# Second step of a graph layer on one core: the finished tile scaled on GpSimd, the threshold guess kept as a logarithm, the last sum taken out earlier

## The chip, the cores and the metric

The kernel runs on one core of a Trainium2 chip. The core has a matrix engine (TensorE, "PE" in the profile), a vector engine (VectorE, "DVE"), a scalar engine (ScalarE, "ACT"), a general engine (GpSimd, "POOL") and a queue that only starts transfers (SyncE, "SP"). Each engine works through its own queue of instructions in order and waits on semaphores for the others. The metric is the time of the whole program on the device in microseconds, as the median of several runs.

## The reference

The layer takes 3327 nodes with 256 features and a sparse adjacency matrix (about 0.12% of the entries, and the diagonal). It normalises the features, mixes them in two steps, adds the result to its input and normalises again. Each step mixes in two ways: `R`, the fixed adjacency with normalised rows, and `A`, a full attention matrix of which every row keeps only its largest entries, those that together hold 90% of the row's sum.

```python
def _top_p_attention(X, W1, W2, W3):
    q = X @ W1.T @ W2.T
    k = X @ W3.T
    probs = softmax(q @ k.T / TAU)
    idx = argsort(-probs)
    sp = take_along_axis(probs, idx)
    cs = cumsum(sp)
    keep_sorted = cs - sp < TOP_P                 # TOP_P = 0.9
    mask = zeros(bool).at[rows, idx].set(keep_sorted)
    A = probs * mask
    return A / maximum(A.sum(-1, keepdims=True), 1e-12)
...
R = S + eye(N);  R = R / R.sum(-1, keepdims=True)
Xf = Xa = X
for n in range(STEPS):                            # STEPS = 2
    A = _top_p_attention(Xa, W1, W2, W3)
    Xf = R @ Xf
    Xa = A @ Xa
    Z = Z + Xf @ U1[n].T + Xa @ U2[n].T
h = X + Z
return (h - mu) / sqrt(var + LN_EPS) * ln_g + ln_b    # mu, var of each row of h
```

The layer's input `X` is `relu(layernorm(x))`, and its output is added to `x`.

## The kernel before, in words

**Tiles.** The 3327 nodes are padded to 3328, which makes 26 tiles of 128 rows. A tile's attention weights `e` are 128 x 3328 in float32, and four to six such tiles lie on the chip at a time. One round of the program works on several tiles, each at another stage; a round of the second step finishes one tile.

**What is done with a tile in the second step.**
- `weights` makes the logits with TensorE (L598) and their exponentials with ScalarE (L602, L606), which also adds up the row sums `Z`.
- `measured_twice` guesses, for each row, a threshold below which the entries hold a little less than a tenth of `Z`. It starts from a first guess `col(9)` out of moments of the row (`guessed`, L618 to L623), and makes three passes of ScalarE over the whole tile (L631, called by `through`): one adds up how far entries lie below the guess, one counts them, and a third counts them below a better guess, `col(13)`. Between these passes stand chains of operations on 128 x 1 columns, spread over ScalarE, VectorE and GpSimd. The better guess is the first one times a factor (L684 to L686). The last guess `col(16)` is `col(13)` times a power (L709, L712); where the measured mass shows that the guess is out of its range (L711), 1e30 is added, so that the proof at the end fails and a slow, exact program runs instead.
- `settle` makes one pass of VectorE that keeps only the entries below `col(16)` (L726), finds the eight largest of each of 20 segments (the scan, twenty MAX8 at L731), sorts the 48 largest of those (L738, L740), finds from their running sum the exact cut (L745 to L750), and makes a second pass of VectorE that sets everything under the cut to zero (L760).
- `Sums` turns the tile round in seven groups of up to four blocks (L806, copied out by ScalarE at L808) and multiplies them with the features `xw` into the accumulator `pa` (L820). There is one buffer for `pa`.
- `diffuse` and `spread` do the sparse mixing with `R`: rows that GpSimd gathers by index (L898, five gathers for a tile), multiplied at L906 and added at L1088.
- `finish` takes `pa` out and adds it to the rest (L930), computes mean and deviation of the rows (L456, L457, L463, L464, L938), scales the tile with ScalarE (L945), multiplies by the gain and adds the bias and the input on GpSimd (L946 to L948), and sends the tile off (L950).

**What sets the order.** The functions are generators, and each `yield` ends a piece. For every round and each of its seven parts, a string of letters in `PLAN` says which generators are moved on by one piece: `d` is `settle` and `c` the same of the tile before; `m` is `measured_twice` of the next tile and `n` of the tile after its round; `s` is `spread`, `f` is `finish`, `g` a gather, `w` and `q` parts of `weights`, `l` the laws of the moments. `OPEN` and `LAST` hold the strings of the first and last rounds. At the end every instruction of PE, ACT, DVE and (in the second step) POOL is tied to the one written ahead of it on its engine, so that the queues keep exactly this order; the SP queue's order is left to the scheduler.

Of the kernel before, what the change touches and what calls it, by code (L numbers as in the profile page):

```python
# [13 lines left out]
AF = mybir.ActivationFunctionType  # L14
ALU = mybir.AluOpType
# [7 lines left out]
NT = (N + P - 1) // P  # L23
# [287 lines left out]


BIG = 1.0e30
SEG = 168
NSEG = -(-NP // SEG)
ROUNDS = (5, 6)
# [27 lines left out]
def guess_graph_layer(ctx, tc, x, adj, w1t, w2t, w3t, u1t, u2t, ln_g, ln_b, out, flag):  # L344
# [15 lines left out]
    V, G, S, PE = nc.vector, nc.gpsimd, nc.scalar, nc.tensor  # L360
# [265 lines left out]
    def con(k):  # L626
        return one[:, k : k + 1]
# [5 lines left out]
    def measured_once(r):  # L633
# [25 lines left out]

        V.tensor_scalar(col(5), oa[:, 1:2], NP - 31.0, BIG, ALU.is_gt, ALU.mult)  # L660
        V.tensor_scalar(col(6), col(4), col(1), 0.35, ALU.mult, ALU.is_lt)
        V.scalar_tensor_tensor(col(5), col(6), BIG, col(5), ALU.mult, ALU.add)
        V.tensor_scalar(col(3), col(3), 1.0e20, col(9), ALU.min, ALU.mult)
        V.tensor_tensor(col(16), col(3), col(5), ALU.add)

    def measured_twice(r):
        e, ms = r["e"], r["ms"]

        col = guessed(r, small.tile([P, 18], F32, tag="g", name="g"))
        S.activation(col(1), col(0), AF.Exp, scale=-1.0, bias=con(5))
        S.activation(col(11), col(2), AF.Square, bias=con(4))  # L673
        G.tensor_scalar(col(11), col(11), ms(5), ms(6), ALU.mult, ALU.add)  # L674
        G.tensor_scalar(col(5), col(1), OFFSET[1], None, ALU.mult)
        yield
        oa = small.tile([P, 3], F32, tag="oa", name="oa")
        through(e, AF.Relu, col(9), -1.0, oa[:, 0:1])
        yield
        through(e, AF.Sign, col(9), -1.0, oa[:, 1:2])  # L680
        yield
        V.tensor_scalar(col(3), oa[:, 1:2], float(NP), col(9), ALU.add, ALU.mult)
        V.tensor_scalar(col(4), col(3), 0.5, oa[:, 0:1], ALU.mult, ALU.subtract)
        S.activation(col(6), col(4), AF.Ln, scale=col(1), bias=con(2))  # L684
        S.activation(col(6), col(6), AF.Exp, scale=col(11))
        S.activation(col(13), col(6), AF.Copy, scale=col(9))  # L686
        G.tensor_scalar(col(14), col(13), col(9), 0.25, ALU.add, ALU.mult)
        G.tensor_scalar(col(10), col(13), col(5), 1.0, ALU.mult, ALU.add)
        G.tensor_scalar(col(8), r["Z"], -0.1, col(4), ALU.mult, ALU.add)
        yield  # L690
        through(e, AF.Sign, col(13), -1.0, oa[:, 2:3])
        yield
        d1 = col(17)
        G.tensor_scalar(col(0), oa[:, 2:3], NP - 61.0, BIG, ALU.is_gt, ALU.mult)
        G.tensor_scalar(col(0), r["Z"], 0.035, col(0), ALU.mult, ALU.add)
        V.tensor_scalar(col(15), oa[:, 2:3], oa[:, 1:2], col(14), ALU.subtract, ALU.mult)
        V.tensor_scalar(d1, col(15), col(4), 0.0, ALU.add, ALU.max)

        S.activation(col(2), d1, AF.Abs, scale=col(1), bias=con(1))
        S.activation(col(2), col(2), AF.Ln, scale=0.2, bias=col(10))  # L700
        S.activation(col(3), d1, AF.Ln, scale=col(1), bias=con(2))
        S.activation(col(2), col(2), AF.Identity, scale=-1.0, bias=col(3))

        V.tensor_scalar(col(12), col(4), d1, 1.0e-30, ALU.subtract, ALU.add)
        V.reciprocal(col(12), col(12))
        G.tensor_scalar(col(12), col(12), col(8), 0.7, ALU.mult, ALU.max)
        G.tensor_scalar(col(11), col(12), 1.5, col(11), ALU.min, ALU.mult)
        yield
        S.activation(col(3), col(2), AF.Exp, scale=col(11))  # L709
        yield  # L710
        V.tensor_scalar(col(6), d1, col(0), BIG, ALU.is_lt, ALU.mult)  # L711
        V.tensor_scalar(col(16), col(3), col(13), col(6), ALU.mult, ALU.add)  # L712

    def measured(step, r):
        return measured_twice(r) if step else measured_once(r)
# [4 lines left out]
    def settle(step, t, r):  # L720
        e, col, Z = r["e"], r["col"], r["Z"]
        n = 8 * ROUNDS[step]
        d2 = small.tile([P, 1], F32, tag="d2", name="d2")
        need = small.tile([P, 1], F32, tag="need", name="need")
        w = scan.tile([P, NP], F32, tag="w", name="w")
        V.scalar_tensor_tensor(w, e, col(16), e, ALU.is_lt, ALU.mult, accum_out=d2)  # L726
        V.tensor_scalar(need, Z, -0.1, d2, ALU.mult, ALU.add)
        yield
        cand = small.tile([P, NSEG * 8], F32, tag="cand", name="cand", bufs=1)
        for s in range(NSEG):  # L730
            V.max(cand[:, 8 * s : 8 * s + 8], w[:, s * SEG : min(NP, (s + 1) * SEG)])  # L731
            if s in (NSEG // 2 - 1, NSEG - 1):
                yield
        at = lambda k: rec[:, step, k, t : t + 1]
        V.tensor_reduce(at(0), cand.rearrange("p (s k) -> p s k", k=8)[:, :, 7], AX.X, ALU.max)
        for k in range(ROUNDS[step]):
            b8 = bb[:, 1 + 8 * k : 9 + 8 * k]
            V.max(b8, cand)  # L738
            if k < ROUNDS[step] - 1:
                V.match_replace(cand, b8, cand, 0.0)  # L740
            if k == 2:
                yield
        b = bb[:, 1 : n + 1]
        cum = small.tile([P, TOPK], F32, tag="cum", name="cum", bufs=1)
        V.tensor_tensor_scan(cum[:, :n], bb[:, :n], bb[:, :n], 0.0, ALU.add, ALU.max)  # L745

        dr = small.tile([P, TOPK], F32, tag="dr", name="dr", bufs=1)
        V.tensor_scalar(dr[:, :n], cum[:, :n], need, None, ALU.is_ge)
        V.scalar_tensor_tensor(cum[:, :n], dr[:, :n], BIG, b, ALU.mult, ALU.add)
        V.tensor_reduce(at(1), cum[:, :n], AX.X, ALU.min)  # L750
        yield
        r["ra"] = ra = small.tile([P, 1], F32, tag="ra", name="ra")
        if t in (0, NT - 1):

            rb = small.tile([P, 1], F32, tag="rb", name="rb", bufs=1)
            for a, b_, r_ in ((0, FIRST, ra), (FIRST, NP, rb)):
                V.scalar_tensor_tensor(e[:, a:b_], e[:, a:b_], at(1), e[:, a:b_], ALU.is_ge, ALU.mult, accum_out=r_)  # L757
            V.tensor_tensor(ra, ra, rb, ALU.add)
        else:
            V.scalar_tensor_tensor(e, e, at(1), e, ALU.is_ge, ALU.mult, accum_out=ra)  # L760
        V.reciprocal(ra, ra)
        yield
        V.tensor_tensor(cum[:, :n], dr[:, :n], b, ALU.mult)
        V.tensor_reduce(at(2), cum[:, :n], AX.X, ALU.max)
# [164 lines left out]
    def finish(t, y, pa, ra):  # L929
        V.scalar_tensor_tensor(y, pa, ra, y, ALU.mult, ALU.add)  # L930
        yield
        mv = spread_of(y)
        yield
        xr = row.tile([P, D], F32, tag="xr", name="xr", bufs=1)
        nc.sync.dma_start(xr, x[t * P : (t + 1) * P])
        rstd = inverse(mv)
        nm = small.tile([P, 1], F32, tag="nm", name="nm")
        G.tensor_scalar(nm, mv[:, 0:1], rstd, -1.0, ALU.mult, ALU.mult)  # L938
        yield
        if t == NT - 1:  # L940
            G.tensor_tensor(xr, xr, bet, ALU.add)
            V.scalar_tensor_tensor(y, y, mv[:, 0:1], gam, ALU.subtract, ALU.mult)
            V.scalar_tensor_tensor(y, y, rstd, xr, ALU.mult, ALU.add)
        else:
            S.activation(y, y, AF.Identity, bias=nm, scale=rstd)  # L945
            G.tensor_tensor(y, y, gam, ALU.mult)  # L946
            G.tensor_tensor(xr, xr, bet, ALU.add)
            G.tensor_tensor(y, y, xr, ALU.add)  # L948
        h = min(P, N - t * P)
        nc.sync.dma_start(out[t * P : t * P + h], y[:h])  # L950
# [143 lines left out]
    def refetch(t):  # L1094
# [7 lines left out]


    PLAN = (("mdsssa", "mcdsssa", "edawwp", "msda", "mpdea", "gdawwq", "emgq"),
            ("llcmss", "lnms", "lwwnfd", "lcmdsssggggg", "fsmwqdf", "llmdf", "lmwd"))

    LAST = {NT - 1: ("cfss", "cn", "nd", "sss", "fdddddsf", "f", ""), NT: ("c", "", "", "ff", "ff", "fv", "f"),
            NT + 1: ("fv", "f", "", "", "f", "f", "f")}
    BEGIN = {-1: ("mba", "mmbba", "mwwbbaa", "bmwwb", "", "", ""),
             0: ("mdbba", "mcdbba", "medbwwbap", "mdabb", "mpdbwwba", "gdabbq", "q"),  # L1110
             1: ("mdsssbba", "mcdsssbba", "edbawwbp", "msdbga", "mpdea", "dawwq", "emgq")}
    OPEN = {-1: ("llcmss", "lnms", "lwwnfd", "lcmdsssggggg", "fmgswqdf", "llmdf", "lmwfdm"),
            0: ("cmssggg", "nms", "wwnfd", "cmdsss", "fsmgwqdf", "mdf", "mwd"),
            1: ("cmss", "nms", "wwnfd", "cmdsssggggg", "fsmwqdf", "mgdf", "mwd")}
    OPEN[2] = OPEN[3] = OPEN[1]
    fetching = itertools.chain(*(refetch(t) for t in range(NT)))
    LATE = (1, 4)
# [5 lines left out]
    for step in range(2):  # L1123
        sums = Sums(step, live, xw if step else x0, AHEAD[step])

        for i in range(-1, NT + 2):
# [4 lines left out]
            if step == 1 and i == -1:  # L1131
# [6 lines left out]
                c=work["d"],  # L1138
                d=settle(step, i, live[step, i]) if valid(i) else none,
                m=measured(step, live[step, i + 1]) if valid(i + 1) else none,  # L1140
                s=spread(step, i - 2 + 2 * step) if valid(i - 2 + 2 * step) else none,
# [97 lines left out]
```

## Time and profile before

| | |
|---|---|
| time before, median of 3 runs | 1396.95 us (1394.01 to 1402.68) |
| the profiled execution: its own time / its span | 1402.92 us / 1401.2 us |
| PE busy | 1276.6 us (91%) |
| DVE busy | 1199.8 us (86%) |
| ACT busy | 1102.5 us (79%) |
| POOL busy | 814.9 us (58%) |
| chain that ended last | DVE 43%, PE 41%, ACT 9% |

The profile is of one execution. A line of a group or of the timeline names the engine, the line of the program, the operation, what it writes and reads with the shapes, and its length; in brackets stands how long the engine stood idle before it and which instruction ended that. A line of the waits names who waited for whom, with the total in microseconds, how many times, and the longest. The chain that ended last is followed back from the last instruction to whatever released it. A busy share is an average over the whole span: the first step and the second differ, and the second, the one that is changed here, runs from about 780 us on.

### The profile page before, as it was taken

The numbers are of one execution on the slowest core, as the hardware profiler recorded it, in microseconds if no ns is written. First come the engines' busy times: TensorE is split into PE (matmuls) and PEld (weight loads), VectorE is DVE, ScalarE is ACT, GpSimd is POOL, SyncE is SP. The second block draws the span as 40 slices with busy tenths as digits, with TensorE's granted clock in tenths as the row PEclk, the third lists the DMA queues.
The fourth block names the chain that finished last, engine by engine and source line by source line (L and its number), as shares of the span: only waits on it lengthen the run. The fifth ranks groups of instructions, "written<-read, shape, count | busy, mean of one in ns | idle before, by whom it ended". The sixth has DMA issues, their size and how long they took to land.

```text
span 1401.2 us, 22108 instructions
## 1 busy us (share of the span) xinstructions
PE 1276.6 (91%) x6495; PEld 976.5 (70%) x6495; DVE 1199.8 (86%) x3689; ACT 1102.5 (79%) x2445; POOL 814.9 (58%) x1244
## 2 busy tenths in 40 slices
PE   5898899999999999999999769999999999999985
PEld 4535777777777777677677547777777777777764
DVE  6878788989999899889882589999998999999984
ACT  5566686778887788778764689999999999999941
POOL 6213888766777667566573475655645556555522
PEclk9999999999999999999999879999999999999998
DMA  8754454453444545444432221221322213122200
GB/s 290 242 167 141 126 153 132 124 148 111 140 142 127 140 117 151 124 126 134 114 82 79 62 63 53 79 84 53 91 61 75 79 58 91 57 79 80 57 20 22
DMA packets 92642, 149.77 MB, mean 107 GB/s; under 512 B 15425, under 2 KB 59072, under 8 KB 92512
## 3 DMA queue, kind: packets, MB, share of 16 engines
q1 hardware_dynamic: 75056, 105.37, 23.9%
q0 software_dynamic: 16640, 42.69, 12.3%
q8 instruction: 54, 0.88, 0.3%
q14 instruction: 76, 0.62, 0.1%
q10 hardware_dynamic: 816, 0.20, 0.1%
HBM read 120.93 MB, written 27.28 MB: 106 GB/s over the span
## 4 chain that ended last, share of the span: by engine, by line
DVE 43%; PE 41%; ACT 9%; issue 5%; POOL 1%; DMA 1%; SPq 0%; DVEq 0%; POOLq 0%; ACTq 0%
PE pa L820 17%; DVE cand L731 9%; DVE w L726 8%; PE pt L806 5%; DVE e L760 5%; PE pl L598 4%; PE pr L906 4%; DVE cand L740 4%; DVE bb L738 3%; PE pz L919 3%; ACT ja L631 3%; DVE x L760 2%; PE pz L987 2%; ACT eT L808 1%; DVE fm L842 1%
## 5 line engine op out<-in xcount | busy, mean ns | idle before, releaser
L820 PE MATMUL pa<-xw,eT 128*128 128x256 f32 x1352 | 324.8, 385 | 27.4 <-DVE s L930 26.2
L631 ACT ACTIVATE ja<-e,g 128x3328 uint8<-128x3328 f32 x106 | 325.8, 3073 | 0.1
L820 PE MATMUL pa<-x,eT 128*128 128x256 f32 x1352 | 324.1, 381 | 0.0
L820 PEld LDWEIGHTS pa<-xw,eT 128*128 128x128 f32 x1352 | 251.6, 191 | 78.2 <-DVE s L930 31.6
L808 ACT COPY eT<-pt 128x512 f32<-128x512 f32 (+1 forms) x364 | 200.7, 559 | 106.5 <-PE pt L806 76.1
L820 PEld LDWEIGHTS pa<-x,eT 128*128 128x128 f32 x1352 | 244.3, 191 | 26.1
L731 DVE MAX8 cand<-w 128x8 f32<-128x168 f32 (+1 forms) x1040 | 251.4, 317 | 0.0
L898 POOL DMA_INDIRECT xg<-bx,index x130 | 165.0, 1269 | 52.0 <-issue 41.6
L806 PE MATMUL pt<-ident,e 128*128 128x128 f32 x1144 | 176.5, 277 | 15.2 <-DVE e L757 9.1
L806 PEld LDWEIGHTS pt<-ident,e 128*128 128x128 f32 x1144 | 141.0, 144 | 55.2 <-issue 27.9
L889 POOL DMA_INDIRECT ac<-in_adj,index x130 | 142.8, 1099 | 43.9 <-issue 29.1
L726 DVE SCALAR_TENSOR_TENSOR w<-e,g 128x3328 f32<-128x3328 f32 x44 | 162.1, 3684 | 0.7
L898 POOL DMA_INDIRECT xg<-vx,index x130 | 129.5, 996 | 38.6 <-issue 38.6
L906 PE MATMUL pr<-xg,ac 128*128 128x257 f32 (+1 forms) x520 | 141.9, 397 | 9.9 <-DVE s L1088 6.3
L760 DVE SCALAR_TENSOR_TENSOR e<-e,rec 128x3328 f32<-128x3328 f32 x40 | 147.7, 3691 | 0.6
L602 ACT ACTIVATE e<-pl 128x832 f32<-128x832 f32 x132 | 113.7, 866 | 16.4 <-PE pl L598 12.0
L906 PEld LDWEIGHTS pr<-xg,ac 128*128 128x128 f32 x520 | 94.2, 195 | 36.4 <-issue 14.6
L738 DVE MAX8 bb<-cand 128x8 f32<-128x160 f32 x286 | 92.6, 324 | 6.7 <-DVE cand L740 0.3
L598 PE MATMUL pl<-both,qT 64*128 64x416 f32 x416 | 91.7, 542 | 6.5 <-DVE e L993 3.5
L598 PE MATMUL pl<-after,qT 64*128 64x416 f32 x416 | 95.9, 555 | 0.0
L842 DVE TENSOR_REDUCE fm<-at 128x4 f32<-128x512 f32 (+1 forms) x133 | 84.5, 635 | 12.8 <-DMA at<-in_adj 11.8
L674 POOL TENSOR_SCALAR g<-g,law 128x1 f32<-128x1 f32 x23 | 46.4, 2016 | 67.1 <-ACT g L673 67.1
(258 smaller groups left out, 2087.3 us busy)
## 6 DMA issues: line engine op xcount, KB each, us to landing
at<-in_adj SPq DMA_DIRECT2D x114, 256.0 KB
cx<-ac SPq DMA_DIRECT2D x26, 384.0 KB
ac<-cx SPq DMA_DIRECT2D x26, 384.0 KB
wide<-in_adj SPq DMA_DIRECT2D x8, 832.0 KB
e<-in_adj SPq DMA_DIRECT2D x6, 832.0 KB
own<-bx SPq DMA_DIRECT2D x26, 128.5 KB
x<-in_x SPq DMA_DIRECT2D x13, 256.0 KB
s<-ax SPq DMA_DIRECT2D x26, 128.0 KB
```

The lines of the kernel that those rows point to most:

```text
L598: PE.matmul(pl[:, a, :wd], qT[p, :], keys_of(step, a).rearrange("p a b -> p (a b)")[:, c : c + wd], start=True, stop=True)
L631: S.activation(ja, e, f, bias=guess, scale=sign, accum_out=total)
L726: V.scalar_tensor_tensor(w, e, col(16), e, ALU.is_lt, ALU.mult, accum_out=d2)
L731: V.max(cand[:, 8 * s : 8 * s + 8], w[:, s * SEG : min(NP, (s + 1) * SEG)])
L738: V.max(b8, cand)
L760: V.scalar_tensor_tensor(e, e, at(1), e, ALU.is_ge, ALU.mult, accum_out=ra)
L806: PE.transpose(pt[:, j, :], e[:, (j0 + j) * P : (j0 + j + 1) * P], ident)
L808: S.copy(eT[:, :w, :], pt[:, :w, :])
L820: PE.matmul(self.pa, eT[:, c - 4 * k, :], self.xa[:, j, :], start=c == 0, stop=c == NT - 1)
L889: G.indirect_dma_start(out=ac[:, k, :], out_offset=None, in_=rows, in_offset=bass.IndirectOffsetOnAxis(ap=index[:, t, k : k + 1], axis=0), ...
L898: G.indirect_dma_start(out=xg[:, k, :w], out_offset=None, in_=rows, in_offset=bass.IndirectOffsetOnAxis(ap=index[:, t, k : k + 1], axis=0))
L906: PE.matmul(pr[:, :w], ac[:, k, :], own if k == KT - 1 else xg[:, k, :w], start=k == 0, stop=k == KT - 1)
```

## The change

The change touches the second step only.

- In `finish`, the scaling of the finished tile goes from ScalarE to GpSimd.
- The better guess `col(13)` comes out of one exponential, whose bias `col(7)` is the logarithm of the first guess. GpSimd computes that bias, and the logarithm of the better guess into `col(6)`.
- The last guess `col(16)` is one exponential on ScalarE with this logarithm as its bias. The guard adds 69 to the logarithm (exp(69) is about 1e30) on GpSimd. The two VectorE operations that made `col(16)` are gone, and a subtraction on ScalarE becomes one on GpSimd.
- The scan of twenty MAX8 gets another `yield` after the first four, so that `finish`'s first piece (L930) stands behind four of them and no longer behind ten.
- One of a tile's five gathers goes from part 3 of the round to its last part.

```diff
+LNBIG = 69.0
...
         G.tensor_scalar(col(5), col(1), OFFSET[1], None, ALU.mult)
+        G.tensor_scalar(col(7), col(3), ms(3), ms(8), ALU.mult, ALU.add)
         yield
...
         S.activation(col(6), col(4), AF.Ln, scale=col(1), bias=con(2))
-        S.activation(col(6), col(6), AF.Exp, scale=col(11))
-        S.activation(col(13), col(6), AF.Copy, scale=col(9))
+        S.activation(col(13), col(6), AF.Exp, scale=col(11), bias=col(7))
         G.tensor_scalar(col(14), col(13), col(9), 0.25, ALU.add, ALU.mult)
         G.tensor_scalar(col(10), col(13), col(5), 1.0, ALU.mult, ALU.add)
         G.tensor_scalar(col(8), r["Z"], -0.1, col(4), ALU.mult, ALU.add)
+        G.tensor_scalar(col(6), col(6), col(11), col(7), ALU.mult, ALU.add)
         yield
...
         S.activation(col(3), d1, AF.Ln, scale=col(1), bias=con(2))
-        S.activation(col(2), col(2), AF.Identity, scale=-1.0, bias=col(3))
 
         V.tensor_scalar(col(12), col(4), d1, 1.0e-30, ALU.subtract, ALU.add)
         V.reciprocal(col(12), col(12))
         G.tensor_scalar(col(12), col(12), col(8), 0.7, ALU.mult, ALU.max)
         G.tensor_scalar(col(11), col(12), 1.5, col(11), ALU.min, ALU.mult)
-        yield
-        S.activation(col(3), col(2), AF.Exp, scale=col(11))
-        yield
-        V.tensor_scalar(col(6), d1, col(0), BIG, ALU.is_lt, ALU.mult)
-        V.tensor_scalar(col(16), col(3), col(13), col(6), ALU.mult, ALU.add)
+        G.tensor_tensor(col(2), col(3), col(2), ALU.subtract)
+        G.tensor_scalar(col(15), d1, col(0), LNBIG, ALU.is_lt, ALU.mult)
+        G.tensor_tensor(col(6), col(6), col(15), ALU.add)
+        yield
+        S.activation(col(16), col(2), AF.Exp, scale=col(11), bias=col(6))
+        yield
...
             V.max(cand[:, 8 * s : 8 * s + 8], w[:, s * SEG : min(NP, (s + 1) * SEG)])
-            if s in (NSEG // 2 - 1, NSEG - 1):
+            if s in (NSEG // 2 - 1, NSEG - 1) or step and s == 3:
                 yield
...
-            S.activation(y, y, AF.Identity, bias=nm, scale=rstd)
+            G.tensor_scalar(y, y, rstd, nm, ALU.mult, ALU.add)
             G.tensor_tensor(y, y, gam, ALU.mult)
...
-            ("llcmss", "lnms", "lwwnfd", "lcmdsssggggg", "fsmwqdf", "llmdf", "lmwd"))
+            ("llcmss", "lnms", "lwwnfd", "lcmdsssgggg", "fdsmwqdf", "llmdf", "lmwdg"))
...
-            1: ("cmss", "nms", "wwnfd", "cmdsssggggg", "fsmwqdf", "mgdf", "mwd")}
+            1: ("cmss", "nms", "wwnfd", "cmdsssgggg", "fdsmwqdf", "mgdf", "mwdg")}
```

The strings of the other first rounds, and of the last one, get the additional `d` in the same way. In the queues, TensorE's order is the same as before; ScalarE's is the same without three operations a tile; in GpSimd's queue, the wide scaling stands just ahead of L946, the operation for `col(7)` behind L675, the one for `col(6)` behind L689, the last three behind L707, and the moved gather behind those. In the SP queue the transfer of `own` (L1078) stands one place earlier, ahead of that of the finished tile.

More of the change, by code (lines that the diff above doesn't have):

```diff
@@ L1104, in guess_graph_layer @@
     PLAN = (("mdsssa", "mcdsssa", "edawwp", "msda", "mpdea", "gdawwq", "emgq"),
-            ("llcmss", "lnms", "lwwnfd", "lcmdsssggggg", "fsmwqdf", "llmdf", "lmwd"))
-    LAST = {NT - 1: ("cfss", "cn", "nd", "sss", "fdddddsf", "f", ""), NT: ("c", "", "", "ff", "ff", "fv", "f"),
+            ("llcmss", "lnms", "lwwnfd", "lcmdsssgggg", "fdsmwqdf", "llmdf", "lmwdg"))
+    LAST = {NT - 1: ("cfss", "cn", "nd", "sss", "fddddddsf", "f", ""), NT: ("c", "", "", "ff", "ff", "fv", "f"),
             NT + 1: ("fv", "f", "", "", "f", "f", "f")}
@@ L1111, in guess_graph_layer @@
              1: ("mdsssbba", "mcdsssbba", "edbawwbp", "msdbga", "mpdea", "dawwq", "emgq")}
-    OPEN = {-1: ("llcmss", "lnms", "lwwnfd", "lcmdsssggggg", "fmgswqdf", "llmdf", "lmwfdm"),
-            0: ("cmssggg", "nms", "wwnfd", "cmdsss", "fsmgwqdf", "mdf", "mwd"),
-            1: ("cmss", "nms", "wwnfd", "cmdsssggggg", "fsmwqdf", "mgdf", "mwd")}
+    OPEN = {-1: ("llcmss", "lnms", "lwwnfd", "lcmdsssggggg", "fmgdswqdf", "llmdf", "lmwfdm"),
+            0: ("cmssggg", "nms", "wwnfd", "cmdsss", "fdsmgwqdf", "mdf", "mwd"),
+            1: ("cmss", "nms", "wwnfd", "cmdsssgggg", "fdsmwqdf", "mgdf", "mwdg")}
     OPEN[2] = OPEN[3] = OPEN[1]
```

## The prediction

> **What bounds the kernel now.** I read the table of windows first, then the chain that ended last in order of time, then the waits of the second step's steady part, then the timeline of one tile. The change touches the second step alone, some 620 of the 1401 us. One window of its steady part (columns: start and end, length, then busy us and instructions of PE, PEld, DVE, ACT, POOL, the TensorE clock, DMA share, GB/s):
>
> ```profile
> 1100.00:1200.00 100.00, 96.30 (x499) 75.44 (x497) 92.51 (x271) 95.77 (x196) 55.31 (x93) 1.00 0.23 67
> ```
>
> Three engines are above 92%; none alone is plainly the bound. The chain says which one paces them:
>
> ```profile
> 1132.22 3.71 DVE w L726 x2
> 1136.91 1.96 DVE cand L731 x8
> 1140.02 2.32 DVE cand L731 x10
> 1149.66 3.71 DVE e L760 x2
> 1154.08 3.71 DVE w L726 x2
> ```
>
> The scan of one tile (L726) starts 21.86 us after that of the tile before, and nearly all the long pieces are DVE's. I count times from that start (1132.22) and call it 0; L760 then starts at 17.44. The waits between 910 and 1304 us, 18 tiles:
>
> ```profile
> POOL s L946 <- ACT s L945: 77.4, 18, 4.4
> ...
> PE pa L820 <- DVE s L930: 16.7, 18, 1.1
> ...
> DVE g L696 <- issue: 10.6, 14, 2.5
> ```
>
> TensorE waits 16.7/18 = 0.93 us in every tile for DVE to take out the last sum (L930), and DVE waits about 0.6 us at L696. The timeline of one tile shows what stands at both places (start, length, engine, line, idle time before in brackets):
>
> ```profile
> 1131.53 0.16 DVE L761 RECIPROCAL ra<-ra 128x1 f32<-128x1 f32 x1
> 1131.61 0.19 DVE L711 TENSOR_SCALAR g<-g 128x1 f32<-128x1 f32 x1
> 1131.91 0.27 DVE L712 TENSOR_SCALAR g<-g 128x1 f32<-128x1 f32 x1
> ...
> 1136.43 2.44 DVE L731 MAX8 cand<-w 128x8 f32<-128x168 f32 x10
> 1138.79 0.47 DVE L930 SCALAR_TENSOR_TENSOR s<-pa,ra,s 128x256 f32<-128x256 f32 x1
> ...
> 1145.80 0.27 DVE L696 TENSOR_SCALAR g<-oa,g 128x1 f32<-128x1 f32 x1 [0.63 <-issue]
> ```
>
> ```profile
> 1139.31 1.99 PE L820 MATMUL pa<-xw,eT 128*128 128x256 f32 x8 [0.92 <-DVE s L930]
> ```
>
> The two operations of the old guess (L711, L712) sit on DVE between its two long passes. DVE's wait at L696 ends when ScalarE's third pass (L631, 1142.52 to 1145.70) has ended.
>
> **GpSimd's queue is the other half.** It is only 55% busy, but its small operations do not run when they like:
>
> ```profile
> 787.23 0.34 POOL L674 TENSOR_SCALAR g<-g,ms 128x1 f32<-128x1 f32 x1 [3.92 <-ACT g L673]
> ...
> 1129.64 2.06 POOL L674 TENSOR_SCALAR g<-g,law 128x1 f32<-128x1 f32 x1 [2.85 <-ACT g L673]
> ...
> 1136.28 0.74 POOL L946 TENSOR_TENSOR s<-s,gam 128x256 f32<-128x256 f32 x1 [4.26 <-ACT s L945]
> ...
> 1148.27 0.30 POOL L707 TENSOR_SCALAR g<-g 128x1 f32<-128x1 f32 x1
> ```
>
> The same L674 takes 0.34 us when no long pass runs and 2.06 us when it meets L760 (1127.80 to 1131.49): it ends 0.2 us after that pass. The blocking goes both ways. Near the end of the step, with L946 to L948 on GpSimd from 1347.53 to 1349.75:
>
> ```profile
> 1347.63 0.67 DVE L748 TENSOR_SCALAR dr<-cum,need 128x48 f32<-128x48 f32 x1
> 1348.34 0.67 DVE L749 SCALAR_TENSOR_TENSOR cum<-dr,bb 128x48 f32<-128x48 f32 x1
> ```
>
> They take 0.25 and 0.21 us elsewhere.
>
> **What the Trainium skill says.** "SBUF — State Buffer", section Who interferes with whom: a VectorE instruction with two SBUF inputs contends with a GpSimd instruction that reads SBUF, and the first to start keeps the shared ports to its end. L726 and L760 read e twice, so they are of this kind; the 2.06 against 0.34 us agree. "GPSIMD Engine Reference", section Elementwise — side-by-side cycle accounting: about 2.6 cycles an element for two tensor inputs, 1.03 for one, at 1.2 GHz. For two inputs the trace agrees: 0.46 to 0.53 us at 128 elements (L886) and 0.73 us at 256 (L948) leave 1.6 to 2.1 ns each. For one wide input no row of before exists. "ScalarE: Activation LUTs", section What ACT_TABLE_LOAD costs: an activation takes 186 ns, 93 ns for each pointer operand and 0.833 ns an element. For L945 that is an estimate of 0.59 us; its row shows 0.61.
>
> **The change part by part, for one tile.**
>
> *DVE.* L711 and L712 go: the next pass can start when L711 did, at 3.83 after L760's start instead of 4.42 (1127.80 to 1131.61, and 1132.22). That is 0.6 us on the pacing engine.
>
> *ScalarE.* L686 goes between L685 and the third pass. L684, L685 and L686 start 0.33 apart because each needs the last, so the third pass ends 0.33 us sooner, at 13.15 instead of 13.48. DVE could be at L696 at 12.95; it starts there at 13.25 instead of 13.58, and 0.3 of the 0.63 us wait stays. L702 (0.21 us of ScalarE's time) and L945 (0.49, 1135.59 to 1136.08) free ScalarE, which is then never late: with L945 gone it reaches L684 about 0.4 us before L683 is done. Those two are worth nothing beyond that cover. The exponential now waits for GpSimd's new sum; queued behind it on ScalarE are the three passes over the next tile, and DVE's L726 waits for it directly.
>
> *The last sum.* L930 moves ahead of six MAX8 of 0.236 us, 1.4 us earlier, to about 5.2. TensorE reaches the waiting matmul 0.93 us too early now, so that stall goes whole. TensorE's own round is then 21.86 − 0.93 = 20.93 us. Does DVE wait there instead? The last matmul of that sum ends 5.0 us after the first transposes behind L760 start (1131.84 to 1136.83), so 5.1 after L760's end; L930 would start 5.4 after it. It holds, by 0.2 to 0.3 us.
>
> Together: L696 at 13.25, L760 3.86 later (1145.80 to 1149.66) at 17.11, the next pass 3.83 later: **20.94 us** for DVE with ScalarE, 20.93 for TensorE. Down 0.92.
>
> *GpSimd* takes five small operations and the wide scaling in each tile, and one of five gathers (1.26 us from start to start) goes behind the new ones. Gathers are not held by a long pass: one at 573.02 took 0.95 us beside L726 from 573.00. The index reads two tiles ahead, so the moved gather has some 20 us. The out transfer waits in the SP queue, with xr and s behind it; the transfer of own now stands before it. All of these are used a tile later, so I cost them at nothing.
>
> What matters is when the last of the row, the sum that writes the new exponent (L711 in the changed text), is done, since ScalarE's exponential waits for it, and the next L726 for that. Now L707 ends at 16.35, 1.1 us before L760. The new row:
> - L675 (the old L674) is held until L760 ends and finishes about 3.9 after its start; L726 now begins at 3.83, so the next two operations, which today fit the gap, are held by L726. The first ends at about 3.8, the new L677 at 4.2.
> - The wide scaling starts at 4.3. Its length d is not in the trace: 0.3 us at the least (any 128x1), 0.73 at the most (two inputs). I take 0.5: 256 × 1.03 / 1.2 ns = 0.22 from the skill plus the 0.25 of a tiny one.
> - From L946's start to the first gather 2.39 us, four gathers 5.0 with the gap: the row of small ones starts at 12.2 (12.0 to 12.5). Today it starts at 12.60.
> - Ten operations take 3.75 us (1144.82 to 1148.57). Fourteen: L711 starts 4.75 after the first, at 16.9 (16.7 to 17.2) and ends at 17.2.
>
> L760 starts at 17.11. So the row ends just ahead of the pass that would shut it out, and L745, L748 and L749, which today meet no GpSimd operation, fall among its last four. Each of the three can be held by at most one of 0.25 us. Bounds: 0 to 0.5 us on DVE (never below 0); I take 0.15.
>
> **Sum.** 20.94 + 0.15 = 21.1 us, 0.76 less. From the first pass (802.79) to the last (1354.32) there are 25 rounds: 25 × 0.76 = 19 us. The start of the step (ScalarE's chain, with the three new operations in place of one) and its end I leave at nothing. The profiled execution took 1402.92 us (span 1401.2 and 1.7 around it), so 1384; it lies 6 above the median of 1396.95, hence **1378 us**.
>
> **The rivals.**
> 1. *The row slips behind L760 in every second tile.* If L711 is 0.2 us later than I say, it is held until L760 has ended. L726 then starts about 0.6 us later than it could (L711, then an exponential of 0.3), and ScalarE's first pass starts some 2.2 us late, of which 0.9 is covered by slack and 1.25 reach L696. That tile takes 21.5 us and the next 22.2, in which L760 is late enough for the row. Mean 21.85: the time of today, about 1397. For it: 0.2 us is all the margin. Against it: [...]L750 (0.24 us, one input) leaves the last operation a slot before L760.
> 2. *Slower: it slips in every tile.* If the scaling or the fourteen operations take over 1.3 us more than I count, the row misses even the late L760. Then the round is one loop: L696 to L760 3.86, the pass 3.7, rest of the row and exponential 0.95, ScalarE to the second L683 point 9.33, to the third pass's end 5.32, and 0.1: 23.25 us, 25 × 1.39 = 35 us more, 1432. If only a third operation slips with every second tile: 22.45 on average, 1412. Against it: no row of before shows a small operation over 0.6 us that met no pass.
> 3. *No contention at all*: 20.94 to 21.0, 1374. For it: the row ends before L745 if d is 0.3.
> 4. *The time goes elsewhere*, for example DVE waits at the earlier L930 for TensorE: 0.3 us a tile given back, 1384.
>
> **How the numbers follow.** My forecast 0.42, rival 3 0.13, rival 4 0.10: together 0.65, 1371 to 1388. Rival 1 0.21, about 1390 to 1403. Rival 2 0.14, 1411 to 1432. Under 1% (14 us) a measurement of this kernel can't be told from no change. Faster, under 1383: 0.60, for part of rival 4 and of the forecast's contention lies above it. Within 1%: 0.26. Slower, above 1411: 0.14. The range for 8 in 10 leaves out rival 2 and a little below: 1370 to 1403; the likeliest case's own is 1371 to 1388.
>
> **What would show it.** Right: L726 starts some 21.1 us apart; no L711/L712 on DVE; TensorE's wait for L930 gone from the list of waits; GpSimd's operation behind the first 128x1 held until L726's end; the small sum done before L760. Wrong: a 128x1 operation of 3 us or more just ahead of the exponential; ScalarE or L726 waiting for GpSimd; L748 or L749 at 0.5 us; DVE idle ahead of L930; the wide scaling over 1 us.

## The result, and the profile after

The changed kernel takes 1379.67 us (median of 4 runs, 1376.15 to 1381.65) against 1396.36 us for the kernel before on the same chip: a ratio of 0.9873, with a 95% interval of 0.9855 to 0.9890 (it is worked out from the single runs; the two medians alone give 0.988). A second measurement of the same pair, last of the experiments, gives 0.9899. The forecast was 1378 us.

The window of the second step's steady part (columns: start and end, length, then busy us and instructions of PE, PEld, DVE, ACT, POOL, the TensorE clock, DMA share, GB/s):

```profile
1100.00:1200.00 100.00, 100.00 (x514) 77.67 (x514) 94.34 (x291) 95.19 (x188) 85.97 (x128) 1.00 0.26 78
```

GpSimd went from 55% to 86% busy, ScalarE's share hardly moved, and TensorE shows no idle time any more. The chain that ended last, in order of time, in two rounds:

```profile
1099.07 3.60 DVE w L728 x2
1109.14 3.07 ACT ja L632 x2
1116.19 3.70 DVE e L762 x2
1120.08 3.60 DVE w L728 x2
1130.15 3.07 ACT ja L632 x2
```

L728 is the old L726 and L762 the old L760. Two scans are now 21.01 us apart; they were 21.86. ("Scan" is used here for the first long pass and what follows it, as in the prediction; "the second long pass" is L762.) The chain now names ScalarE's third pass (L632). Before, it showed 0.56 us of "issue" at that place (1145.17 in the profile before), the wait that the prediction reads as one for the third pass (by time: that pass was read out at 1145.70, and L696 started at 1145.80). So the path through ScalarE isn't new; the profile now names it. In other stretches, from 960 to 1004 us for example, the chain runs over GpSimd's queue, so that queue too is close to the path. The waits between 910 and 1290 us:

```profile
POOL g L675 <- ACT g L674: 8.7, 17, 1.4
...
ACT g L686 <- DVE g L685: 7.5, 17, 0.4
DVE g L698 <- ACT ja L632: 6.5, 16, 0.7
```

TensorE's wait for the last sum is gone from the list, and so is GpSimd's wait for the scaled tile. VectorE still waits 0.4 us for ScalarE's third pass. One tile in VectorE's timeline:

```profile
1103.17 1.03 DVE L733 MAX8 cand<-w 128x8 f32<-128x168 f32 x4
1104.12 0.46 DVE L932 SCALAR_TENSOR_TENSOR s<-pa,ra,s 128x256 f32<-128x256 f32 x1
...
1112.30 0.28 DVE L698 TENSOR_SCALAR g<-oa,g 128x1 f32<-128x1 f32 x1 [0.39 <-ACT ja L632]
...
1116.19 3.68 DVE L762 SCALAR_TENSOR_TENSOR e<-e,rec 128x3328 f32<-128x3328 f32 x1
1119.80 0.08 DVE L762 DVE_READ_ACCUMULATOR e<-e,rec 128x1 f32 x1
1119.92 0.16 DVE L763 RECIPROCAL ra<-ra 128x1 f32<-128x1 f32 x1
1120.00 3.67 DVE L728 SCALAR_TENSOR_TENSOR w<-e,g 128x3328 f32<-128x3328 f32 x1
```

The two passes now stand 3.81 us apart, and the last sum (L932) is behind four pieces of the scan. GpSimd's timeline of the same tile:

```profile
1096.68 2.39 POOL L675 TENSOR_SCALAR g<-g,law 128x1 f32<-128x1 f32 x1 [0.42 <-ACT g L674]
1099.14 3.60 POOL L676 TENSOR_SCALAR g<-g 128x1 f32<-128x1 f32 x1
1102.82 0.42 POOL L677 TENSOR_SCALAR g<-g,law 128x1 f32<-128x1 f32 x1
1103.21 0.55 POOL L947 TENSOR_SCALAR s<-s,rstd,nm 128x256 f32<-128x256 f32 x1
...
1111.07 0.26 POOL L688 TENSOR_SCALAR g<-g 128x1 f32<-128x1 f32 x1
...
1115.80 0.19 POOL L711 TENSOR_TENSOR g<-g 128x1 f32<-128x1 f32 x1
1116.16 1.13 POOL L900 DMA_INDIRECT xg<-vx,index  x1 [0.17 <-issue]
```

L675 is held by one long pass and L676 by the next. The row of small operations, from L688 to L711 ("the row" below), ends at 1115.99, 0.2 us before the pass at 1116.19.

Between the first and the last scan lie 533.2 us, against 551.5 before: 18.3 less. The first scan begins at 798.12 instead of 802.79, and from the last scan to the end it takes 0.6 us longer; together this makes the 22.4 us between the two profiled spans. The 4.7 us ahead of the first scan lie where both programs are the same. They are not put down to the change: among four kernels that were measured side by side, all with this first step, the first scan starts anywhere from 774 to 781 us.

In 2 of the 25 rounds, the fourth and the twelfth, the row did miss the pass. The fourth, from the timeline:

```profile
878.50 3.69 DVE L762 SCALAR_TENSOR_TENSOR e<-e,rec 128x3328 f32<-128x3328 f32 x1
...
878.69 3.54 POOL L709 TENSOR_TENSOR g<-g 128x1 f32<-128x1 f32 x1
...
882.60 0.19 POOL L711 TENSOR_TENSOR g<-g 128x1 f32<-128x1 f32 x1
...
882.82 0.39 ACT L713 ACTIVATE g<-g 128x1 f32<-128x1 f32 x1 [2.65 <-POOL g L711]
...
883.24 3.91 DVE L728 SCALAR_TENSOR_TENSOR w<-x,g 128x3328 f32<-128x3328 f32 x1 [0.85 <-ACT g L713]
```

The exponential waits 2.65 us and the scan 0.85. This round took 21.91 us and the one after it 22.50. What is different in that round can be seen: the strings of the opening rounds (`mgdf` in `OPEN`) put one more gather into the row itself, here at 874.85 for 0.99 us. In the twelfth round a gather starts 2.6 us late (see the last section).

### The profile page after: what moved, and what is told of

The parts are those of the page before. It is cut to its first block, busy times and chain, and to the rows that moved or that the text cites. A ratio compares the mean times of both kernels' runs of the same rounds, so it can differ in the third digit from the quotient of the medians.

```text
span 1378.8 us, 22108 instructions
## 1 busy us (share of the span) xinstructions
PE 1279.0 (93%) x6495; PEld 975.2 (71%) x6495; DVE 1188.6 (86%) x3637; ACT 1079.2 (78%) x2368; POOL 954.0 (69%) x1399
## 4 chain that ended last, share of the span: by engine, by line
PE 42%; DVE 26%; ACT 18%; POOL 7%; issue 4%; DMA 2%; SPq 0%; another core or an unknown queue 0%; ACTq 0%; DVEq 0%; POOLq 0%
PE pa L822 18%; ACT ja L632 7%; PE pt L808 5%; DVE w L728 5%; PE pr L908 5%; DVE cand L733 5%; PE pl L599 4%; DVE e L762 3%; PE pz L921 3%; ACT eT L810 2%; PE pz L989 2%; DVE bb L740 2%; DVE cand L742 2%; POOL xg L900 2%; ACT e L603 1%
## 5 line engine op out<-in xcount | busy, mean ns | idle before, releaser
L632 ACT ACTIVATE ja<-e,g 128x3328 uint8<-128x3328 f32 x106 | 325.7, 3073 | 0.1
L891 POOL DMA_INDIRECT ac<-in_adj,index x130 | 148.2, 1140 | 43.9 <-issue 29.4
L728 DVE SCALAR_TENSOR_TENSOR w<-e,g 128x3328 f32<-128x3328 f32 x44 | 162.1, 3684 | 2.7 <-ACT g L713 2.7
L900 POOL DMA_INDIRECT xg<-vx,index x130 | 133.4, 1026 | 34.1 <-issue 29.4
L762 DVE SCALAR_TENSOR_TENSOR e<-e,rec 128x3328 f32<-128x3328 f32 x40 | 147.9, 3697 | 0.6
L676 POOL TENSOR_SCALAR g<-g 128x1 f32<-128x1 f32 x26 | 73.4, 2823 | 1.7
```

Of the source, the lines that this page charges most:

```text
L632: S.activation(ja, e, f, bias=guess, scale=sign, accum_out=total)
L891: G.indirect_dma_start(out=ac[:, k, :], out_offset=None, in_=rows, in_offset=bass.IndirectOffsetOnAxis(ap=index[:, t, k : k + 1], axis=0), ...
L900: G.indirect_dma_start(out=xg[:, k, :w], out_offset=None, in_=rows, in_offset=bass.IndirectOffsetOnAxis(ap=index[:, t, k : k + 1], axis=0))
```

## The experiments

After the result my theory was that VectorE together with ScalarE's third pass paces the round, that TensorE's wait for the last sum was slack, and that GpSimd's row matters only by whether it ends before the second long pass. The rivals were that TensorE's removed stall made the gain, that ScalarE's relief made it, or that GpSimd is off the path. "Round" below is the median distance between two starts of the scan in the run's timeline. The runs were made in several groups and on more than one chip. In these the kernel before took from 1376 to 1405 us, on one and the same chip 1376 and 1395, so ratios to the kernel before in the same group and rounds are compared, not times. Most of that difference lies in the first step (the first scan starts anywhere from 774 to 803 us); the rounds agree: 21.86 and 21.85 us before and with the last sum alone, 21.01 and 21.05 for the changed kernel, each from two groups. Of changed strings only those of `PLAN` are shown; `OPEN` and `LAST` follow, and where new columns are used their tile is made wider. Added lines shift the line numbers behind them.

**The last sum alone.** The kernel before with this:

```diff
-            if s in (NSEG // 2 - 1, NSEG - 1):
+            if s in (NSEG // 2 - 1, NSEG - 1) or step and s == 3:
...
-  "fsmwqdf"
+  "fdsmwqdf"
```

> The kernel before with nothing but the last sum moved ahead of six of the scan's first ten pieces. My theory: the round of the second step is set by VectorE together with ScalarE (21.86 us before), and the 0.93 us for which TensorE waited for the last sum in every tile was slack of TensorE. The wait disappears from that line and turns up elsewhere on TensorE; the round stays at 21.86 us, the time within 3 us of before (ratio 0.998 to 1.002). Rival (the stall of TensorE was the bound): the round falls by 0.5 to 0.93 us, the time by 12 to 22 us, to 1374 to 1384.

Ratio 0.9987 (0.9978 to 0.9996), round 21.85 us. In the waits between 900 and 1270 us, TensorE's wait has moved to another place:

```profile
PE pt L806 <- DVE e L760: 7.5, 11, 0.7
```

It now comes to the transposes behind the long pass too early, by about 0.68 us in a steady round instead of 0.92. In the steady round the stall at the last sum was slack. Taking it away alone is worth about 0.1%, at the edge of what can be told, and the profiles show where: in the last round of the step, which took 25.56 us before and takes 23.13 here (one other round, the thirteenth, is 0.95 us longer).

**The last sum back in its old place**, in the changed kernel (the reverse of the diff above):

> The changed kernel with the last sum back behind ten pieces. My theory: TensorE meets the last sum late again by some 0.1 to 0.5 us and is late by as much at its next transposes, but its own work is 20.93 us of a round of 21.02, so the round becomes 21.0 to 21.1 us and the time 1379 to 1384 (ratio to before 0.987 to 0.991). Rival (TensorE's stall is paid in full): the round goes back to 21.5 to 21.9 us, the time to 1391 to 1397.

Ratio 0.9885 (0.9869 to 0.9902), round 21.06 us. The changed kernel's rounds are 21.01 us in its first profile and 21.05 in its second. So this part costs or gains at most 0.05 us in a steady round. The last round takes 24.77 us instead of 22.12, which fits the last round of the run above: there the early sum pays. Why it does was not tried.

**The scaling back on ScalarE**, in the changed kernel:

```diff
-            G.tensor_scalar(y, y, rstd, nm, ALU.mult, ALU.add)
+            S.activation(y, y, AF.Identity, bias=nm, scale=rstd)
```

> The changed kernel with the finished tile scaled on ScalarE again. My theory: ScalarE waits 0.44 us in each round for the counts of VectorE, and the scaling takes about 0.49 us there, so ScalarE reaches that point about as late as VectorE does: round 21.0 to 21.1 us, time 1379 to 1383 (ratio 0.987 to 0.990). Rival (ScalarE's relief is what made the gain): the round grows by the whole 0.49 us, 12 us more, 1392.

Ratio 0.9900 (0.9884 to 0.9917), round 21.17 us, a little above the range. The scaling fills ScalarE's wait for the counts, and about 0.15 us of it sticks out.

**Both of these back**, so that only the logarithm and the moved gather are left:

> The changed kernel with the scaling back on ScalarE and the last sum back behind ten pieces: what is left of the change is the guess kept as a logarithm and the moved gather. My theory: nearly the whole gain comes from these: round 21.15 to 21.3 us, ratio to before 0.989 to 0.993. Rival (the parts only work together, TensorE's stall or ScalarE's time comes back in full): round 21.5 us or more, ratio 0.995 or more.

Ratio 0.9930 (0.9905 to 0.9954). The rounds take 21.15 to 21.2 and 21.4 us in turn, some 21.28 on average, and TensorE's wait for the last sum (L932) is back. Of the 0.85 us a round, 0.58 are left with the logarithm and the moved gather alone. The other two parts are each worth little when the rest is in place, and 0.27 together. In time, 0.7% of a gain of 1.0 to 1.3% is left.

**The two operations back on VectorE.** The changed kernel, with two gathers behind the row (see below) and this between the two passes:

```diff
+        if step:
+            V.tensor_scalar(col(18), col(16), 1.0, None, ALU.mult)
+            V.tensor_scalar(col(19), col(18), 1.0, None, ALU.mult)
-        V.scalar_tensor_tensor(w, e, col(16), e, ALU.is_lt, ALU.mult, accum_out=d2)
+        V.scalar_tensor_tensor(w, e, col(19 if step else 16), e, ALU.is_lt, ALU.mult, accum_out=d2)
```

> The changed kernel with two gathers behind GpSimd's row, and with two 128x1 operations, each waiting for the one ahead of it, put back on VectorE between its two long passes (they copy the threshold). My theory: they cost what they cost before, 0.6 us in every round, since VectorE paces the round: 21.6 us, 25 x 0.6 = 15 us, ratio to before 0.994 to 0.998. Rival (they are covered, as TensorE is busy nearly all the time): 21.0 us, ratio 0.985.

Ratio 0.9916 (0.9884 to 0.9947), round 21.38 us, 0.40 above the 20.98 of the same kernel without them. Their lines (L729 and L730; the scan is L731 here):

```profile
1117.65 0.13 DVE L729 TENSOR_SCALAR g<-g 128x1 f32<-128x1 f32 x1
1117.82 0.15 DVE L730 TENSOR_SCALAR g<-g 128x1 f32<-128x1 f32 x1
1118.01 3.69 DVE L731 SCALAR_TENSOR_TENSOR w<-e,g 128x3328 f32<-128x3328 f32 x1
```

They are cheaper than those that the change removed (0.13 and 0.15 against 0.19 and 0.27 us), and they are paid in full: 0.36 us from the first to the scan. The size of my expectation (0.6 us) was off, the mechanism held. The two are not the old operations: they have no pointer operands, and so they show that time between the passes is paid, not what the old pair cost.

**One more operation on ScalarE**, in the changed kernel with two gathers behind the row:

```diff
-        S.activation(col(13), col(6), AF.Exp, scale=col(11), bias=col(7))
+        S.activation(col(18), col(6), AF.Exp, scale=col(11), bias=col(7))
+        S.activation(col(13), col(18), AF.Copy)
```

> The changed kernel with two gathers behind GpSimd's row, and with one more operation on ScalarE after the one exponential of the better guess: a copy that waits for it, in the place of the old multiplication. My theory: ScalarE's third pass, for which VectorE waits 0.39 us in each round, ends 0.2 to 0.33 us later, and the round grows by as much: 21.2 to 21.3 us, ratio to before 0.988 to 0.992. Rival (ScalarE's other waits cover it): 21.0 us, ratio 0.985.

Ratio 0.9909 (0.9880 to 0.9937), round 21.23 us, 0.25 more. ScalarE's part of the guess is on the path: VectorE and ScalarE's third pass form one loop, and time added to either is paid.

**All five gathers ahead of the row**, in the changed kernel:

```diff
-  "lcmdsssgggg", "fdsmwqdf", "llmdf", "lmwdg"
+  "lcmdsssggggg", "fdsmwqdf", "llmdf", "lmwd"
```

> The changed kernel with all five gathers in one place again, ahead of GpSimd's row of small operations. My theory: the row starts 1.26 us later, its last two or three operations are held by the second long pass of VectorE (3.6 us), and the exponential of ScalarE and the next scan wait for them: rounds of about 21.5 to 21.9 and 22.2 to 22.5 us in turn, mean about 22, time 1396 to 1405. Rival (GpSimd is off the path): round 21.0 us, 1380.

Ratio 1.0053 (1.0034 to 1.0072): slower than before. The rounds take 22.18 and 22.50 us in turn. The waits between 900 and 1270 us show the missed pass, in nine of the rounds:

```profile
ACT g L713 <- POOL g L711: 22.7, 9, 2.5
```

The mean of 22.3 us is near what I expected, the shape is not: the first of the two rounds has a second loss, for VectorE now also waits 0.78 us at L698 (0.39 in the changed kernel), where it needs the first result of GpSimd's row. (By time: that operation, L688, ends at 1123.01 in one such round and L698 starts at 1123.05, while the third pass was over at 1122.55. The list of waits names other instructions for most of these waits.)

**One more operation in the row**, in the changed kernel:

```diff
+        G.tensor_scalar(col(18), col(11), 1.0, None, ALU.mult)
         G.tensor_tensor(col(2), col(3), col(2), ALU.subtract)
```

> The changed kernel with one more 128x1 operation on GpSimd (its result is not used), in the row just ahead of the subtraction. My theory: the row's last operation ends 0.2 us before the second long pass of VectorE begins; 0.3 to 0.4 us more pushes it behind, and it is held by that pass in about every second round: mean round 21.6 to 22.0 us, time 1392 to 1402. Rival (small delays of GpSimd are absorbed, since the three small two-input operations of VectorE ahead of the pass wait their turn): round 21.0 to 21.2, 1380 to 1385.

Ratio 0.9937 (0.9916 to 0.9958). Rounds of 20.98, 21.39 and 22.51 us follow one another, 21.63 on average: with 0.4 us more on GpSimd, every third round misses the pass, not every second as I expected. In one that does (L712 is the row's last operation here):

```profile
1097.43 0.31 POOL L711 TENSOR_SCALAR g<-g 128x1 f32<-128x1 f32 x1
1097.83 3.39 POOL L712 TENSOR_TENSOR g<-g 128x1 f32<-128x1 f32 x1
```

The pass there began at 1097.46. So the margin of 0.2 us is real, and about half of the gain in time hangs on it.

**Six more operations in the row** (the same line six times):

> The changed kernel with six more 128x1 operations on GpSimd in the row, 1.6 to 2.2 us (results not used). My theory: the row misses the second long pass in every round and the round becomes one loop of VectorE's passes, the row's rest, the exponential and ScalarE's three passes: 23.0 to 23.6 us, time 1425 to 1440. Rival (a slip only ever costs every second round): 22 us, 1400 to 1408.

Ratio 1.0185 (1.0165 to 1.0205), round 22.91 us, in nearly every round the same. The row misses the pass every time, as the theory says. The loop is a little shorter than I worked out, because only the row's last operation (L713 here) is caught by the pass and ends with it, so that from the pass's end only the exponential stands ahead of the next scan (0.5 us, where I had counted 0.95):

```profile
1119.76 0.30 POOL L712 TENSOR_SCALAR g<-g 128x1 f32<-128x1 f32 x1
1120.14 3.39 POOL L713 TENSOR_TENSOR g<-g 128x1 f32<-128x1 f32 x1
```

**Two gathers behind the row**, in the changed kernel:

```diff
-  "lcmdsssgggg", "fdsmwqdf", "llmdf", "lmwdg"
+  "lcmdsssggg", "fdsmwqdf", "llmdf", "lmwdgg"
```

> The changed kernel with two of the five gathers behind the row of small operations instead of one. My theory: the row starts 1.26 us sooner and has over 1 us to spare before the second long pass, so the rounds in which it slipped after a disturbance (two in the trace of the changed kernel, at some 0.9 and 1.5 us each, and the late rounds after them) go; the steady round of 21.02 us stays, since VectorE with ScalarE sets it. 1375 to 1378 (ratio 0.985 to 0.987). Rival: the slips cost nothing that counts, 1380; or two gathers ahead of the next tile's first operation delay that one and what follows, 1382 or more.

Ratio 0.9850 (0.9830 to 0.9870), round 20.98 us. The early slip is gone (the fourth and fifth rounds take 21.04 and 21.03 us, where the changed kernel took 21.91 and 22.50); the other, in the twelfth round behind the late gather, is not, though I expected both to go. The row now ends 1.1 us ahead of the pass, and the steady round moves by 0.03 us only: in a steady round GpSimd's queue doesn't set the pace.

**The counts ahead of the sparse sum**, on top of that:

```diff
-  "fdsmwqdf"
+  "fdmswqdf"
```

> The changed kernel with two gathers behind GpSimd's row, and with VectorE's two operations on the counts (which ScalarE waits for by 0.44 us) ahead of the addition of the sparse sum. My theory: ScalarE's third pass ends 0.4 us sooner and VectorE's wait of 0.39 us for it goes, so VectorE with ScalarE could run a round in 20.6 us; but TensorE's own work of 20.9 us now sets it: round 20.9 us, ratio to before 0.982 to 0.985. Rival (TensorE is not yet the bound): round 20.6, ratio 0.976 to 0.979. Second rival (the later sparse sum holds TensorE up): 21.0 or more, 0.985.

Ratio 0.9844 (0.9817 to 0.9871), round 20.86 us. VectorE's wait at L698 is gone in steady rounds, and the round still does not fall below 20.7 to 20.9. What sets it now is probably TensorE. Its busy share can't tell, for it is 100% in the changed kernel as well, but the chain that ended last runs over TensorE alone from 1159 to 1205 us, where before it ran over VectorE and ScalarE (in the run with two gathers behind the row):

```profile
1160.40 0.87 PE pt L808 x8
1161.27 1.60 PE pl L599 x8
...
1177.82 3.45 PE pa L822 x16
1181.27 0.87 PE pt L808 x8
```

No run takes work off TensorE, so this isn't shown by an experiment. The round also lies below the 20.93 us that the prediction worked out as TensorE's own. The ratio's interval overlaps that of the run above, and both those of the changed kernel, so that only the rounds tell these apart.

**The changed kernel once more**, beside the last ones:

> The changed kernel itself once more, beside the others of this row and the kernel before. Ratio to before as on record, 0.985 to 0.989; median round 21.0 us with one or two slips of GpSimd's row.

Ratio 0.9899 (0.9865 to 0.9933), round 21.05 us. The ratio is a little above the range that I gave; the two intervals of the changed kernel overlap.

## Why the prediction was right

- *VectorE's two operations.* Predicted 3.83 us from pass to pass, measured 3.81 (the two times that the prediction gives in brackets, 1127.80 and 1131.61, are 3.81 apart too). That time at this place is paid in full is shown by putting two operations there again.
- *ScalarE.* The third pass was to end at 13.15 us after the scan's start and did at 13.21 (1112.19 less 1098.98); VectorE's wait left over was to be 0.3 and is 0.39. The term that was mis-sized is the exponential: it has two pointer operands now, and takes 0.39 us where L685 took 0.29. (Nor did L684, L685 and L686 all start 0.33 apart: from L684 to L685 it was 0.48, since L684 has two pointer operands as well.) "ScalarE: Activation LUTs" of the Trainium skill, section What ACT_TABLE_LOAD costs, gives 93 ns for each pointer operand, and this case agrees. I had quoted the page and not applied it here.
- *The last sum.* That TensorE's stall goes was right. I let it stand beside VectorE's saving as if both were needed, and did not say that the stall was slack as long as VectorE took 21.86 us. Done alone it brings 0.13%, and undone alone it costs at most 0.05 us in a steady round. What it is worth lies in the step's last round, which I had left at nothing.
- *The scaling.* I gave it nothing beyond cover. It is worth about 0.15 us a round, since on ScalarE it fills the whole wait for the counts and a little more.
- *GpSimd's row.* Start predicted 12.2, measured 12.09 (1111.07); L711 predicted to start at 16.9, measured 16.82. I wrote that the row ends just ahead of L760, but my own numbers hardly say so: an end at 17.2 against a pass at 17.11, or at 17.26 with the 0.15 us that I added. Measured were 17.01 and 17.21. That the row makes it in nearly every round was more than the sum could promise, and so in part luck. The wide scaling takes 0.55 us; the estimate from "GPSIMD Engine Reference", section Elementwise — side-by-side cycle accounting, was 0.5.
- *The price of two engines holding each other.* I took 0.15 us on VectorE. From L698 to the pass it took 3.89 us instead of 3.86: nearly nothing. This error and the exponential's cancel in part, and the steady round came out at 21.01 for 21.1: the mechanism was right, that it came so near was in part luck.
- *Where the row misses the pass.* I made this rival 1, for every second round. It happened in two rounds. The sum of 19 us left this out, and it left out the ends of the step; the 18.3 measured come near it because these errors cancel. 25 x 0.85 would be 21.2 us. The fourth, fifth and thirteenth rounds, which slip or follow a slip, take 3.9 us more than steady ones; the last round, on the other side, fell from 25.56 to 22.12, 2.6 us more than a steady round; smaller differences in the first rounds and in the tenth, twelfth and twenty-first make up the rest. My price for a missed round and the next (21.5 and 22.2) was too low; they take 21.4 to 22.2 and 22.5, and with all gathers ahead of the row the kernel is slower than before, not equal to it. Rival 2's loop of 23.25 us was measured at 22.91.
- *The other rivals.* Rival 3, no contention, comes nearest to the steady round (20.94 to 21.0). Rival 4 did not come about: L932 stands in VectorE's timeline without idle time before it.
- *A false step that did no harm.* I said that a long pass does not hold a gather, from a single row (573.02). It does: see the last section. The moved gather escapes because it starts about 0.03 us ahead of the pass; that it does is luck again.

## What to carry to other kernels

When several engines are all above 90%, look for the loop that closes, not for the busiest engine or the longest wait: here a wait of 0.92 us in every round, taken from an engine with time to spare, came back at that engine's next meeting point for 0.68 us and left the round as it was. Work moved to an engine with idle time still has a time by which it must be done; draw its queue against the long instructions that shut it out, and keep more than a fraction of a microsecond between. Here a gather moved behind the row was a cheap way to buy that room: with all five ahead of it the whole gain was lost.

## What the runs showed of the hardware that was not expected

A gather that GpSimd issues while VectorE is in a pass that reads its tile twice is held past the pass's end; it ends about 0.8 us after it. In the run with two gathers behind the row, the pass runs from 1068.35 to 1072.04; the first gather starts ahead of it and takes 1.12 us, the second starts within it:

```profile
1067.39 1.12 POOL L900 DMA_INDIRECT xg<-vx,index  x1 [0.17 <-issue]
1068.82 4.04 POOL L900 DMA_INDIRECT xg<-vx,index  x1 [0.31 <-issue]
```

The kernel before has 20 such gathers of 2.4 to 4.4 us, all but one in its first step; those that start no later than about 0.1 us after a pass's start mostly take 0.95. "SBUF — State Buffer" of the Trainium skill, section Who interferes with whom, says that descriptor generation waits for VectorE's two-port modes, and infers from a probe that an operation with two inputs does not hold it; here the passes do have two inputs, and the gather took 4.04 us. The two need not contradict each other: the gather takes its rows' numbers from `index`, a tile in SBUF (the memory on the chip), so it may fall under the sentence on GpSimd instructions that read SBUF, which the prediction takes from the same section. Whether the reading of the index waits or the writing of descriptors, no run here tells apart.

In the profiles of the kernel before, of the changed one and of several others, one gather of the twelfth round waits about 2.6 us (for TensorE, by the list of waits of the changed kernel), and the round takes 22.4 us or more. Why this happens there and in no other round was not tried and stays open.
